# Masks of the closing products from memory and ScalarE instead of ScalarE and GpSimd, in a four-layer graph network

## The chip, the cores and the metric

The kernel runs on one core of one Trainium2 chip. The metric is device time in microseconds. Three runs of the kernel before gave 1397.5, 1397.81 and 1398.58 us; the median is 1397.81.

Each core has a matrix engine (TensorE, PE in the profile, with its weight loads as PEld), VectorE (DVE), ScalarE (ACT), GpSimd (POOL) and SyncE (SP), which here issues the memory transfers. Each engine works through its own queue.

## What is computed

Eight graphs (batches) of 2048 nodes with 64 features pass four layers. They share one adjacency matrix. Layers 0 to 2 are graph attention; each ends in a residual sum and a normalization of every row. Layer 3, the one that the change touches, is attention that works feature by feature:

```python
feat = jax.nn.softplus(x * (INV_SQRT2 * w0[0, 0]) + b0[0])
scores = feat * wa + ba
mask = adj > 0
logits = scores[:, None, :, :] * mask[None, :, :, None].astype(scores.dtype)
logits = jnp.where(mask[None, :, :, None], logits, jnp.float32(-1000000000.0))
attn = jax.nn.softmax(logits, axis=2)
out = jnp.einsum('bijd,bjd->bid', attn, feat)
...
x = _layernorm(x + _L3_gnn_ref(x, L3_gnn_w0, L3_gnn_b0, L3_gnn_wa, L3_gnn_ba, adj), axis=-1)
```

The score of a pair (i, j) depends on j alone, so with d = exp(scores) the output is (mask @ (feat * d)) / (mask @ d): two products of the 0/1 adjacency mask with a narrow matrix.

## The kernel before

**Tiling.** The 2048 nodes are K = 16 blocks of 128. Layers 0 to 2 are worked off as 24 units, one for each layer and batch, in the order of the list `todo`; the last eight are layer 2, and "the last unit" below is layer 2 of batch 7 (named `2_7` in the code). A unit has 16 steps `jb`. In each, VectorE makes a 128 x 2048 tile of weights, ScalarE takes its exponential in layer 2, and TensorE multiplies it.

**Layer 3.** Batches go by pairs (m = 0 to 3). `l3_features(b)` makes the two operands of a batch: softplus on ScalarE (absolute value, exp, log, relu), an addition and the sum `fs` on VectorE, d on GpSimd and ScalarE, then `v`, which holds each operand as a rounded part (copied by ScalarE) and the remainder (subtracted by GpSimd for the first batch of a pair, by VectorE for the second). `l3_products` then works through 64 blocks: block = 16 m + ib is the rows ib of the pair m. A block is 32 matmuls: 16 steps jb times the two parts of `v`, with a 128 x 128 tile of the mask as the stationary operand. ScalarE moves each result from PSUM into `nd`. After every second block `l3_finish` loads the residual (`e`), divides, adds, normalizes and stores to `out`.

**Where the masks come from.** The adjacency lies on chip in eight bits as `edge` (16 x 2048 columns on each partition). The products want it in float32. `mask_out`, from unit 9 on, writes the whole mask in float32 to a buffer in memory, `mask_d`. For blocks 0 to 32, which run beside the units of layer 2, `widen(block)` asks for four quarters, and `fetch()`, called after every fourth step of a block, issues one transfer of 256 KB for a quarter into one of five buffers `mask`. For blocks 33 to 63, behind the last unit (`now[0] == 3`), `widen` casts `edge` on chip into one of two buffers `row`: on ScalarE for even blocks, on GpSimd for odd ones. `widen(block + 1)` is called at the start of `block`, just behind the `nd` of block - 1.

**Order.** PE, VectorE, ScalarE and GpSimd run in the order in which the code issues their instructions (class `InOrder`). The code is a set of generators; `Streams.step` runs each of them to its next `yield`. `l3_products` yields twice in a block, so a block takes two steps, and the steps of the other streams fall between its halves. Behind the last unit these streams are its `finish`, `l3_features` of batches 6 and 7, and `l3_finish` of earlier blocks. SP's transfers are not held to that order: the framework places them in SP's queue.

Of the kernel before, what the change touches and what calls it, by code (L numbers as in the profile page):

```python
# [50 lines left out]
def gnn4_kernel(ctx: ExitStack, tc: tile.TileContext, t, out):  # L51
# [55 lines left out]
    class Banks:  # L107
# [4 lines left out]
        pool = None  # L112
# [28 lines left out]
    pe, dve, act, pool = (InOrder(e) for e in (nc.tensor, nc.vector, nc.scalar, nc.gpsimd))  # L141
# [74 lines left out]
    src = t["L0_gnn_a"]  # L216
# [947 lines left out]
    now = [0, 0, 0]  # L1164
# [82 lines left out]
    def widen(block):  # L1247

        if block >= K * B // 2:
            return  # L1250
        ib = block % K
        src = edge[:, :, ib * P : (ib + 1) * P]
        if now[0] == 3:
            m = work.tile([P, K, P], F32R, tag="row", name=f"mask_{block}")
            if block % 2:
                pool.tensor_copy(m, src)
            else:
                act.copy(m, src)
            wide[block] = [m[:, r * K8 : (r + 1) * K8] for r in range(4)]
            return  # L1260
        wide[block] = [None] * 4
        asked.extend((block, r) for r in range(4))
# [11 lines left out]
    def l3_products():  # L1274

        while len(pairs) == 0 or not hasattr(pairs[0], "v"):
            yield 1
        widen(0)
        for _ in range(4):
            fetch()  # L1280
# [3 lines left out]
        for block in range(K * B // 2):  # L1284
            m, ib = divmod(block, K)
            while len(pairs) <= m or pairs[m].ready < 2:
                yield 1
            q = pairs[m]
            widen(block + 1)
            if ib % K4 == 0:  # L1290
                yield from nd_slots.take()
# [707 lines left out]
```

## Time and profile before

The profiled execution took 1401.63 us, of which the instructions span 1399.8. It is a single execution, 3.8 us above the median of the three timed runs. Times inside the profile count from the start of the span.

| stretch, us | PE busy | DVE busy | ACT busy | POOL busy | granted PE clock | GB/s |
|---|---|---|---|---|---|---|
| 1200 to 1220 | 20.00 | 17.96 | 12.91 | 18.15 | 1.00 | 148 |
| 1220 to 1240 | 15.72 | 10.42 | 16.65 | 11.95 | 0.99 | 88 |
| 1240 to 1260 | 16.54 | 19.36 | 9.43 | 16.02 | 0.84 | 24 |
| 1260 to 1280 | 13.81 | 14.96 | 5.97 | 11.45 | 0.83 | 43 |
| 1280 to 1300 | 12.81 | 16.91 | 12.77 | 14.66 | 0.91 | 21 |
| 1300 to 1320 | 20.00 | 17.37 | 6.98 | 12.14 | 0.91 | 41 |
| 1340 to 1360 | 20.00 | 15.46 | 7.66 | 14.06 | 1.00 | 33 |
| 1380 to 1400 | 5.72 | 11.18 | 1.67 | 7.36 | 0.74 | 34 |

The sums of the last unit end at about 1230.6 us. The table shows four stretches in turn: layer 2 and layer 3 together with PE full; from 1230 to 1300 the last unit's own finish and the features of batches 6 and 7, with PE partly idle; from 1300 to 1386 the products alone with PE full again; and a tail in which the last rows are finished. Over the whole span PE is busy 87%, DVE 86%, ACT 59%, POOL 55%.

All operations of the four compute engines have one line in the profile (L80, the helper that issues them), so instructions are told apart by their tiles. `p_l` is a product of layer 3, `p_o` one of a unit's finish, `p_fm` one with `fs`, `acc` one of an attention unit. `st`, `isw`, `o`, `den`, `nd` and `e` are tiles of finishing; a trailing `_x` marks those of the attention layers.

### The profile page before, as it was taken

The numbers are of one execution on the slowest core, as the hardware profiler recorded it, in microseconds if no ns is written. First come the engines' busy times: TensorE is split into PE (matmuls) and PEld (weight loads), VectorE is DVE, ScalarE is ACT, GpSimd is POOL, SyncE is SP. The second block draws the span as 40 slices with busy tenths as digits, with TensorE's granted clock in tenths as the row PEclk, the third lists the DMA queues.
The fourth block names the chain that finished last, engine by engine and source line by source line (L and its number), as shares of the span: only waits on it lengthen the run. The fifth ranks groups of instructions, "written<-read, shape, count | busy, mean of one in ns | idle before, by whom it ended". The sixth has DMA issues, their size and how long they took to land.

```text
span 1399.8 us, 19531 instructions
## 1 busy us (share of the span) xinstructions
PE 1220.0 (87%) x7169; PEld 624.2 (45%) x7169; DVE 1208.8 (86%) x1108; ACT 821.6 (59%) x1593; POOL 770.2 (55%) x1075
## 2 busy tenths in 40 slices
PE   3699888999898988999997879799989999976995
PEld 3333233333343333333332324256645565666995
DVE  3889889999997999889998888998879798877876
ACT  3444543666646753555547996868666758664432
POOL 1666776546765663645542342443555564776664
PEclk8699999999999999999999988999999899998998
DMA  8640000000000221222101000034543444511111
GB/s 291 228 95 1 1 2 1 1 2 1 3 1 1 91 76 47 78 74 93 32 1 39 1 15 1 22 94 129 146 122 92 127 119 138 160 28 33 35 38 34
DMA packets 112010, 87.24 MB, mean 62 GB/s; under 512 B 57917, under 2 KB 90845, under 8 KB 110882
## 3 DMA queue, kind: packets, MB, share of 16 engines
q1 hardware_dynamic: 111538, 85.79, 20.9%
q8 instruction: 59, 0.97, 0.3%
q14 instruction: 45, 0.37, 0.1%
q10 hardware_dynamic: 368, 0.12, 0.0%
HBM read 60.40 MB, written 25.45 MB: 61 GB/s over the span
## 4 chain that ended last, share of the span: by engine, by line
PE 49%; DVE 24%; ACT 11%; issue 7%; POOL 6%; DMA 2%; SPq 1%; ACTq 0%; DVEq 0%; POOLq 0%
PE acc L80 26%; DVE w L80 16%; PE p_l L80 14%; ACT w L80 2%; PE p_o L80 2%; ACT x L80 2%; DVE o L80 1%; PE r L80 1%; PE p_s L80 1%; POOL sq_x L80 1%; DMA raw<-in_adjT_dram 1%; DVE nd L80 1%; POOL st_x L80 1%; DVE edge L80 1%; ACT y L80 1%
## 5 line engine op out<-in xcount | busy, mean ns | idle before, releaser
L80 DVE SCALAR_TENSOR_TENSOR w<-r,se,edge 128x2048 f32<-128x2048 f32 (+1 forms) x270 | 552.9, 2102 | 30.9 <-PE r L80 22.6
L80 PE MATMUL acc<-w,pv 128*64 128x512 f32 x2048 | 494.1, 615 | 53.0 <-DVE w L80 39.4
L80 DVE SCALAR_TENSOR_TENSOR w<-r,lo_g,edge 128x2048 f32<-128x2048 f32 (+1 forms) x144 | 297.8, 2096 | 26.0 <-PE r L80 12.4
L80 ACT ACTIVATE w<-w,down_g 128x2048 f32<-128x2048 f32 (+1 forms) x144 | 256.8, 1808 | 64.6 <-DVE w L80 57.4
L80 PEld LDWEIGHTS p_l<-v,mask 128*128 128x128 f32 x2048 | 256.3, 196 | 61.8 <-issue 48.5
L80 PE MATMUL p_l<-v,mask 128*128 128x256 f32 x2048 | 271.1, 291 | 10.6 <-POOL mask L80 7.0
L80 PE MATMUL acc<-w,x 128*64 128x512 f32 x1024 | 261.8, 640 | 19.2 <-ACT w L80 16.3
L80 PEld LDWEIGHTS acc<-w,pv 128*64 128x64 f32 x2048 | 132.6, 139 | 307.6 <-issue 182.4
L80 POOL TENSOR_TENSOR sq_x<-sq_x 128x32 f32<-128x32 f32 (+4 forms) x207 | 110.1, 532 | 63.8 <-ACT sq_x L80 49.3
L80 PEld LDWEIGHTS acc<-w,x 128*64 128x64 f32 x1024 | 66.5, 143 | 138.9 <-issue 86.6
L80 ACT ACTIVATE x<-o,st_x 128x64 f32<-128x64 f32 x256 | 91.5, 445 | 13.2 <-POOL st_x L80 13.2
L80 ACT ACTIVATE nd<-p_l,empty 128x256 f32<-128x256 f32 x64 | 30.2, 471 | 109.1 <-PE p_l L80 109.1
L80 ACT ACTIVATE o<-p_o,den 128x64 f32<-128x64 f32 x256 | 55.8, 323 | 47.0 <-DVE den L80 47.0
L80 PE MATMUL p_o<-rh,oT 128*128 128x130 f32 x384 | 61.9, 298 | 24.4 <-DVE o L80 6.7
L80 PEld LDWEIGHTS p_o<-rh,oT 128*128 128x128 f32 x384 | 50.2, 197 | 58.3 <-issue 32.3
L80 ACT COPY oT<-acc 128x512 f32<-128x512 f32 x48 | 25.7, 587 | 80.8 <-PE acc L80 80.8
L80 POOL TENSOR_TENSOR st_x<-isw_x,mhalf 128x16 f32<-128x16 f32 x24 | 70.5, 2938 | 1.9
L80 POOL TENSOR_TENSOR eh<-eh,x 128x1024 f32<-128x1024 f32 (+2 forms) x24 | 36.5, 1532 | 47.0 <-ACT eh L80 47.0
L80 DVE RECIPROCAL nd<-nd 128x256 f32<-128x256 f32 x32 | 55.7, 1742 | 0.0
L80 POOL TENSOR_TENSOR d<-x,wa_bc 128x1024 f32<-128x1024 f32 x8 | 19.0, 2379 | 66.5 <-DVE x L80 66.5
L80 POOL TENSOR_TENSOR sq_x<-o 128x512 f32<-128x512 f32 x23 | 29.3, 1273 | 34.6 <-DVE o L80 34.1
L80 ACT ACTIVATE xs<-x,nodes 128x64 f32<-128x64 f32 x128 | 44.7, 434 | 3.2 <-PE p_xT L80 3.2
(258 smaller groups left out, 1523.5 us busy)
## 6 DMA issues: line engine op xcount, KB each, us to landing
mask<-mask_d SPq DMA_DIRECT2D x132, 256.0 KB
mask_d<-mf SPq DMA_DIRECT2D x32, 512.0 KB
raw<-in_adjT_dram SPq DMA_DIRECT2D x8, 1024.0 KB
raw<-in_adjT_dram SPq DMA_DIRECT2D x16, 512.0 KB
x<-in_x_dram SPq DMA_DIRECT2D x8, 512.0 KB
x_d<-x SPq DMA_DIRECT2D x8, 512.0 KB
e<-x_d SPq DMA_DIRECT2D x64, 64.0 KB
out_dram<-o SPq DMA_DIRECT2D x64, 64.0 KB
```

Of the source, the lines that this page charges most:

```text
L80: ins = f(*args, **kwargs)
```

## The change

Behind the last unit, only odd blocks are cast, and by ScalarE. Even blocks fall through to the four quarters from memory, as blocks 0 to 32 do. So of blocks 33 to 63, the sixteen odd ones move from GpSimd to ScalarE and the fifteen even ones from ScalarE to 60 transfers of 256 KB. `mask_d` holds the whole mask already. The buffers stay as they are: five of `mask`, two of `row`.

```diff
@@ -1250,12 +1250,9 @@
             return
         ib = block % K
         src = edge[:, :, ib * P : (ib + 1) * P]
-        if now[0] == 3:
+        if now[0] == 3 and block % 2:
             m = work.tile([P, K, P], F32R, tag="row", name=f"mask_{block}")
-            if block % 2:
-                pool.tensor_copy(m, src)
-            else:
-                act.copy(m, src)
+            act.copy(m, src)
             wide[block] = [m[:, r * K8 : (r + 1) * K8] for r in range(4)]
             return
         wide[block] = [None] * 4
```

## The prediction

> **What bounds the kernel now.** I read the page, then the chain of waits, then PE's waits and the timelines behind the last unit, where alone the change acts. The chain ends so:
>
> ```profile
> 1297.65 1.80 ACT mask L80
> 1299.49 86.24 PE p_l L80 x704
> ```
>
> From 1299.49 us on TensorE multiplies without a break: 704 matmuls are 22 blocks of 32 (blocks 42 to 63). Then a tail of 14.0 us (1385.8 to 1399.8) finishes the last rows. So PE's work is the bound there, and whatever lets those blocks begin earlier shortens the program. Block 42 was released by a ScalarE cast. Before it, from 1230 to 1300 us, PE waits (columns: total us, times, longest):
>
> ```profile
> PE p_l L80 <- POOL mask L80: 7.0, 2, 6.2
> PE p_o L80 <- DVE st L80: 5.7, 1, 5.7
> PE p_fm L80 <- DVE fs L80: 4.0, 1, 4.0
> PE p_l L80 <- ACT mask L80: 2.3, 1, 2.3
> ```
>
> Casts stand for 9.3 us of the 19 shown, but those 9.3 us are not on offer: PE's queue is in order, and the p_o and p_fm products of the last unit and of batch 6 sit between the blocks. The timeline of PE (start, length, instruction, idle before) shows what lies where:
>
> ```profile
> 1252.24 9.83 PE L80 MATMUL p_l<-v,mask 128*128 128x256 f32 x80
> 1268.26 14.15 PE L80 MATMUL p_l<-v,mask 128*128 128x256 f32 x96 [6.19 <-POOL mask L80]
> 1286.43 0.43 PE L80 MATMUL p_fm<-fs,ones 128*128 128x64 f32 x2 [4.01 <-DVE fs L80]
> 1286.67 5.55 PE L80 MATMUL p_l<-v,mask 128*128 128x256 f32 x32
> 1293.05 4.10 PE L80 MATMUL p_l<-v,mask 128*128 128x256 f32 x32 [0.83 <-POOL mask L80]
> ```
>
> Rows 1 and 2 are blocks 34 (half) to 36 and 37 to 39; p_fm stands before block 40; the last two rows are blocks 40 and 41. Blocks 37 to 39 can come 6 us earlier and PE then only waits longer at p_fm, which needs the sum fs of batch 7's features. So the real chain behind the last unit is not PE but the features of batch 7 on DVE, ACT and POOL.
>
> What the masks cost (min/median/max ns):
>
> ```profile
> L1269 SPq DMA_DIRECT2D mask<-mask_d x132: 319/320/774, 744.5 to 1225.7; - x132
> L80 POOL CAST mask<-edge x16: 1884/1892/2092, 1237.1 to 1378.1; 128x2048 fp32r<-128x2048 fp8e4 x16
> L80 ACT CAST mask<-edge x15: 1882/1889/1896, 1238.6 to 1374.6; 128x2048 fp32r<-128x2048 fp8e4 x15
> ```
>
> ScalarE and GpSimd take the same 1.89 us; it is the place in the queue that differs.
>
> **What the Trainium skill says.** "SBUF — State Buffer", Who interferes with whom: VectorE and GpSimd share a port pair under an exclusive lock, and a VectorE instruction with two SBUF inputs blocks for as long as a GpSimd instruction that reads SBUF runs. The trace agrees: this operation on 16 columns ends with the GpSimd cast of block 37 (1266.33 to 1268.21), while its like in the steady stretch (st, 4 columns) takes 0.15 to 0.25:
>
> ```profile
> 1266.40 1.84 DVE L80 SCALAR_TENSOR_TENSOR st_x<-st_x 128x16 f32<-128x16 f32 x1 [2.37 <-POOL st_x L80]
> 1274.92 2.07 DVE L80 TENSOR_TENSOR o<-o,e 128x256 f32<-128x256 f32 x1
> ```
>
> The second row (0.42 elsewhere) lies under the cast of block 39. "TensorE: Matmul & The Clock Gate", Part 1: after an idle window of some 3.4 us the clock falls to half until PE has been busy as long. The trace has 0.50 granted after the gaps before 1242.7, 1268.3 and 1286.4, and even after the 2.35 us gap before block 42 (1301 to 1304.2): 1.6 us lost each time or more. "DMA: Bandwidth & Descriptors", Anatomy of one DMA: a semaphore wait of a DMA is held on the issuing sequencer, so a fetch queues behind whatever SP waits for; the waits of SP's out_dram issues here are up to 9.1 us.
>
> **The change part by part.** Block 43 is the place to count to, since behind it nothing but PE binds. The order on each engine follows from the streams: one step runs every stream to its next yield, and a block takes two steps.
>
> 1. Fifteen even casts leave ACT (15 x 1.89 = 28 us), sixteen odd ones leave POOL (16 x 1.89 = 30 us) and come onto ACT at their places, just behind the nd of the block two before. Sixty fetches (15 x 4) go onto SP, 0.32 us to issue: 19 us over 150 us of a mostly idle queue. For a landing I have the lone quarter issued at 1225.70: its bytes flow from about 1226.8 to 1228.4, so it lands after 2.7 us, and I take 1.5 us more for each quarter behind it.
>
> 2. Blocks 33 to 36: cast 33 lands behind Relu (ends 1238.2) and is done at 1240.1, before the p_o that holds PE to 1242.67: no cost. Cast 35 runs 1250.5 to 1252.4 and pushes the v copies of batch 6 by 1.89, but POOL was to use them only at 1253.7: nothing. Quarters of 34 at the worst are issued behind the out of 1245.46, at 1246.4, and land from 1249.1 to 1253.6, needed from 1249.95 to 1253.2: 0.4 at most, which point 3 takes up.
>
> 3. Blocks 37 to 39: mask 37 is on ACT behind nd of 35 (1258.3), done 1260.5 instead of 1268.2, so PE runs through and is done with 39 at about 1275. This is given back at p_fm at once. It also pays for any late quarter of 36 or 38 (up to 2 us if SP holds them behind an out): that costs nothing.
>
> 4. The chain to batch 7's features. st_x above loses its blocking: 1.84 to 0.16, gain 1.7. Then o, x_7, the reduction, reciprocal and o follow as before; the add under cast 39 loses 1.6 of its 2.07 and its wait on POOL: done at 1273.85 instead of 1276.99. ScalarE's first softplus, which takes the buffer this add frees, moves from 1277.02 to 1273.9, and fs, hence p_fm, from 1286.43 to 1283.3: 3.1 us. The DVE product under cast 41 (1.85 instead of 0.42) gives 1.4 more: x_7 times d ends at 1290.5 instead of 1295.07, the v copies of batch 7 end at 1292.7 instead of 1297.7.
>
> 5. Block 40 starts at 1283.5, cold after 8 us of idling: 3.84 at full clock plus about 2.2, to 1289.6. Block 41 (its cast is done at 1282.7) to 1293.4. Block 42, from memory, to 1297.3. Its quarters, if behind the e load of 1289.3, land 1292.8 to 1297.3: at most 1.0 late, and hidden by the next wait.
>
> 6. The new wait is block 43. Its cast was on POOL at 1299.05; on ACT it stands behind this one and the nd of block 41:
>
> ```profile
> 1302.65 0.42 ACT L80 ACTIVATE sq<-o 128x256 f32<-128x256 f32 x1 [3.21 <-DVE o L80]
> 1302.97 0.46 ACT L80 ACTIVATE nd<-p_l,empty 128x256 f32<-128x256 f32 x1
> ```
>
> sq waits for DVE's o, which follows four v differences (0.63 to 0.68 each without blocking; the fourth took 2.38 under cast 43). After the copies of 1292.7 and a reciprocal to 1293.3 these end at 1296.0, o at 1296.9, sq 1297.3, nd 1297.75, cast 43 at 1299.65, PE at 1299.8. Block 43 thus starts where 42 started before (1299.49). Before, 42 ended and 43 began at 1305.06. That is 5.3 us gained at full clock. The gap of 2.5 us ahead of 43 equals the one that half-clocked PE before; a second 1.6 us would leave 3.7.
>
> 7. Steady blocks (3.84 us, 7.68 per pair). An odd cast is done 2.3 us after the block two before ends, needed at 3.84: hidden, 1.5 us to spare. Fetches of block 62, say, follow the e load (1369.19, pushed by 1.9 since sq now stands behind a cast; DVE idles 1.78 there and is unblocked by 0.6 per pair): q0 issued 1372, q3 at 1373.3 when its buffer (five deep) is free, landed from 1374.7 to 1379.2, needed from 1378.1 to 1381. Hidden, 1.8 us to spare at the least; without that cover it is up to 2.7 us a pair. The tail keeps its 14 us: the next to last sq waits for nd of block 63 anyway.
>
> Sum: 5.3 less 1.6 with odds of somewhat better than even, plus up to 0.7 from the unblocking of isw under cast 35 earlier in the chain: 4.2 us. The profiled execution is then 1401.63 - 4.2 = 1397.4 (span 1395.6). It stands 3.8 above the median of 1397.81, which I move by the same amount: 1393.6.
>
> **The rivals.**
> - A, more gain: block 43 doesn't wait (sq is ready earlier than I count) and PE goes 40 to 63 without a break; 43 starts at 1297.3, gain 7.8: 1390.0. For it: DVE's rows are full of blocked operations that I shortened only in part. Against it: the v copies and the reciprocal are before sq in any case.
> - B, no effect: PE's lost gap comes back as half clock twice, or the chain is longer by the casts that ACT took over; gain 0 to 2.8, about 1396.5.
> - C, slower: SP holds the fetches. If the queue has each pair's out before the fetches, an out at 1375.28 + 1.9 lets q0 go at 1378.1 and land at 1380.8 against 1378.1, 2.7 us late, on ten even blocks 44 to 62: 27 us less 4.2 is 23 slower, 1420; with 0.8 us each, 1401.5. It decides from 0.42 us a block. For it: SP is in order and its outs wait long. Against it: in the last unit fetches and outs interleave on SP and no wait of PE's for a mask from memory appears; SP's order follows readiness rather than the code (batch 7's store is issued at 1270.66, ahead of the out at 1273.96 that precedes it in the code); in the code's order the fetches are ahead of that out as well.
>
> **How the numbers follow.** The forecast 0.58, A 0.13, B 0.15, C 0.14. About 0.2% (2.8 us) is what a measurement here can tell. The forecast's own range is 1392 to 1395.5. The range asked for reaches over A and B and the near end of C: 1389.0 to 1399.5. Faster by over 0.2%: A and most of the forecast, 0.68. Within: B and the forecast's edge, 0.18. Slower: C, 0.14.
>
> **What would show it.** Right: no wait of PE for POOL; one wait of 4 to 9 us at p_fm, near 1283; a wait of some 2 us for ACT's mask ahead of block 43 near 1300; 21 unbroken blocks behind it; st_x near 0.2 us; the tail at 14 us. Wrong: a wait of PE for a DMA in every second block (C); or p_fm still near 1286, so that the port lock was not what held DVE; or no wait at 43 (A).

## The result, and the profile after

Timed side by side, 22 runs each, the changed kernel has a median of 1395.55 us and the kernel before 1398.03. The ratio of the two sets of runs is 0.9984, 95% interval [0.997, 0.9998], or 2.2 us less (0.3 to 4.2). The forecast was 1393.6 within 1389.0 to 1399.5. A second set of runs, told below, gave 0.9964 [0.9952, 0.9976]. Single runs of either kernel lie anywhere from about 1389 to 1406 us, so the medians need many runs, and the profiles say more than one time does.

The two profiled executions span 1399.8 and 1397.1 us. The code is the same up to the end of the last unit's sums, yet that point lies at 1230.55 us before and at 1231.70 after. From here on I count from it, as +x. Behind it the change took the stretch to the end of the span from 169.25 to 165.4 us: 3.85 less.

The masks (min/median/max ns, first and last start) show that the change is in force: 60 more fetches, none on GpSimd.

```profile
L1266 SPq DMA_DIRECT2D mask<-mask_d x192: 319/320/1020, 744.8 to 1370.9; - x192
L80 ACT CAST mask<-edge x16: 1883/1888/1894, 1239.3 to 1376.1; 128x2048 fp32r<-128x2048 fp8e4 x16
```

PE's waits behind 1230 us (total, times, longest). No wait for GpSimd, none for a mask from memory; one long wait at p_fm, and one for a cast of ScalarE:

```profile
PE p_fm L80 <- DMA e<-x_d: 10.3, 1, 10.3
PE p_o L80 <- DVE st L80: 5.2, 1, 5.2
PE p_l L80 <- ACT mask L80: 2.6, 1, 2.6
...
```

The profile names a load as what p_fm waited for, since that landed last; but p_fm multiplies fs, and the chain below has fs end at 1284.68, just ahead of p_fm at 1284.73. PE's timeline:

```profile
1252.90 21.55 PE L80 MATMUL p_l<-v,mask 128*128 128x256 f32 x176
1284.73 0.69 PE L80 MATMUL p_fm<-fs,ones 128*128 128x64 f32 x2 [10.29 <-DMA e<-x_d]
1285.18 13.21 PE L80 MATMUL p_l<-v,mask 128*128 128x256 f32 x96
1301.01 29.23 PE L80 MATMUL p_l<-v,mask 128*128 128x256 f32 x229 [2.62 <-ACT mask L80]
```

Row 1 is block 34 (half) to 39 without a break; before, 6.2 us were lost in it. They come back in row 2: PE waits 10.3 us at p_fm instead of 4.0. Row 3 is blocks 40 to 42, and block 43 starts in row 4 behind the new wait (the row is cut off where the window shown ends). The chain of waits (start, length, what), which up to the v differences ran through the same places before; there it went on through ScalarE's v copies and `nd` to the cast of block 42:

```profile
1268.02 0.17 DVE st_x L80
...
1281.49 1.23 DVE x L80
1282.74 1.94 DVE fs L80
...
1294.46 2.97 DVE v L80 x4
1297.43 0.35 DVE o L80
1297.87 0.43 DVE o L80
1298.39 0.42 ACT sq L80
1298.81 0.36 ACT nd L80
1299.17 1.79 ACT mask L80
1301.01 82.39 PE p_l L80 x672
```

672 matmuls are blocks 43 to 63: PE is unbroken from one block later than before (there 704, from block 42). Block 43 starts at +69.3, where block 42 started before (+68.9); that is one block of 3.84 us less 0.4. The rest of the 3.85 us lies in the tail behind PE, 13.7 us instead of 14.1. The two VectorE operations that lay under GpSimd's casts are short now (1.84 and 2.07 us before):

```profile
1268.02 0.17 DVE L80 SCALAR_TENSOR_TENSOR st_x<-st_x 128x16 f32<-128x16 f32 x1 [2.37 <-POOL st_x L80]
...
1274.86 0.42 DVE L80 TENSOR_TENSOR o<-o,e 128x256 f32<-128x256 f32 x1
```

These two account for the whole: from the start of st_x to the end of fs the chain took 19.97 us before (1266.40 to 1286.37) and takes 16.66 now (1268.02 to 1284.68), 3.3 us less, and the two operations are shorter by 1.67 and 1.65.

### The profile page after: what moved, and what is told of

Read it like the earlier page. It is cut to its first block, busy times and chain, and to the rows that moved or that the text cites. A ratio compares the mean times of both kernels' runs of the same rounds, so it can differ in the third digit from the quotient of the medians.

```text
span 1397.1 us, 19649 instructions
## 1 busy us (share of the span) xinstructions
PE 1220.7 (87%) x7169; PEld 621.7 (45%) x7169; DVE 1194.6 (86%) x1108; ACT 823.1 (59%) x1594; POOL 735.1 (53%) x1059
## 4 chain that ended last, share of the span: by engine, by line
PE 48%; DVE 24%; ACT 12%; POOL 7%; issue 7%; DMA 2%; SPq 0%; DVEq 0%; POOLq 0%; ACTq 0%
PE acc L80 26%; DVE w L80 16%; PE p_l L80 14%; ACT w L80 3%; PE p_o L80 2%; ACT x L80 2%; DMA raw<-in_adjT_dram 2%; PE r L80 1%; PE p_s L80 1%; DVE o L80 1%; POOL sq_x L80 1%; DVE nd L80 1%; ACT y L80 1%; POOL st_x L80 1%; PE p_h L80 1%
## 5 line engine op out<-in xcount | busy, mean ns | idle before, releaser
L80 PE MATMUL acc<-w,x 128*64 128x512 f32 x1024 | 265.3, 648 | 17.8 <-ACT w L80 15.0
L80 POOL TENSOR_TENSOR st_x<-isw_x,mhalf 128x16 f32<-128x16 f32 x24 | 70.5, 2937 | 1.9
L80 POOL TENSOR_SCALAR isw<-isw 128x4 f32<-128x4 f32 x32 | 8.8, 274 | 105.0 <-DVE isw L80 91.2
L80 DVE RECIPROCAL nd<-nd 128x256 f32<-128x256 f32 x32 | 55.7, 1742 | 0.0
```

What stands on the lines that cost most here:

```text
L80: ins = f(*args, **kwargs)
```

## The experiments

The theory: GpSimd's casts kept VectorE waiting in the chain of batch 7's features, and with that chain shorter the end is set by cast 43 on ScalarE. The rivals: that memory is what pays, by freeing ScalarE; that PE's idle time itself is what costs; that fetches come too late. All kernels below are the changed one with an edit. The stretch is from one profile each, and in the three kernels that were profiled twice it moved by 0.7 to 0.8 us; the ratio, with its interval, is to runs of the kernel before on the same chip.

| kernel | p_fm | stretch, us | ratio to before |
|---|---|---|---|
| before | +55.9 | 169.25 | |
| before, second profile | +55.75 | 168.5 | |
| the change | +53.0 | 165.4 | 0.9984 [0.997, 0.9998] |
| the change, second set | +53.3 | 164.6 | 0.9964 [0.9952, 0.9976] |
| e1: odd on GpSimd | +55.7 | 166.9 | 0.9976 [0.9963, 0.9989] |
| e2: all on ScalarE | +53.2 | 163.3 | 0.9959 [0.9941, 0.9977] |
| e3: 33 to 47 from memory | +53.3 | 175.2 | 1.0032 [1.0019, 1.0045] |
| e4: all from memory | +55.2 | 188.3 | 1.0129 [1.0102, 1.0157] |
| e5: p_fm late | - | 166.2 | 1.0 [0.9989, 1.0011] |
| e7: casts ahead | +52.7 | 161.5 | 0.997 [0.995, 0.9989] |
| e8: p_fm late, 41 and 43 from memory | - | 167.6 | 1.0032 [1.0021, 1.0044] |
| e9: casts ahead, p_fm late | - | 161.5 | 0.9946 [0.992, 0.9973] |
| e9, second set | - | 160.8 | 0.9939 [0.9923, 0.9955] |

The ratios follow the stretches only roughly. e5 and e8 have a shorter stretch than the kernel before, yet e5 is no faster in the timed runs and e8 is slower; the profiled execution of e8 (1393.14 us) is the fastest of its six. What each experiment says of the order of events is read from its profile.

**e1_pool_odd: is it GpSimd's casting or the fetching?**

```diff
-            act.copy(m, src)
+            pool.tensor_copy(m, src)
```

> Even blocks from memory as in the change, odd ones cast by GpSimd as before. Times are counted from the end of the last unit's sums (before: 1230.5 us in the profile, after: 1231.7), where the stretch to the end of the span was 169.3 us before and 165.4 after, and the wait of PE's p_fm ended at +55.9 before and +53.0 after. Theory (the port lock): VectorE is blocked by the casts of blocks 37, 39 and 41 again, st_x takes about 1.8 us, p_fm comes back to about +55.9; block 43 is then released by GpSimd's cast near +70.5 and the stretch is 166 to 168. Rival (the masks from memory alone bring the gain, by taking the cast of block 42 off ScalarE): p_fm stays near +53 and the stretch is 165.4 or less.

Measured: p_fm at +55.7, block 43 at +70.5, stretch 166.9, all three as the theory had it. With GpSimd casting odd blocks, the old length of st_x is back, and PE's waits for GpSimd with it. VectorE's and PE's rows of this kernel:

```profile
1267.71 1.84 DVE L80 SCALAR_TENSOR_TENSOR st_x<-st_x 128x16 f32<-128x16 f32 x1 [2.37 <-POOL st_x L80]
```

```profile
1287.58 0.43 PE L80 MATMUL p_fm<-fs,ones 128*128 128x64 f32 x2 [3.85 <-DVE fs L80]
...
1294.23 7.93 PE L80 MATMUL p_l<-v,mask 128*128 128x256 f32 x64 [0.86 <-POOL mask L80]
1302.39 6.97 PE L80 MATMUL p_l<-v,mask 128*128 128x256 f32 x56 [0.22 <-POOL mask L80]
```

So it is GpSimd's casts that hold p_fm back, with the fetches there or not. Yet this kernel too is faster than before, since block 42 no longer waits for ScalarE and cast 43 stood early enough on GpSimd. The two halves of the change overlap: fetching alone brings 2.3 us of stretch, the whole change 3.85. The difference between e1 and the change is seen in the profiles alone; the timed runs (0.9976 against 0.9984 and 0.9964) do not tell the two apart.

**e2_act_all: is memory needed?**

```diff
-        if now[0] == 3 and block % 2:
+        if now[0] == 3:
```

> No fetch behind the last unit: ScalarE casts odd and even blocks. Theory: the gain of the change is GpSimd casting none; ScalarE has room for both, cast 42 stands behind the copies of batch 7 and ends about 2 us late for PE, but cast 43 is released by the same step of VectorE as in the change, so the stretch from the end of the last unit's sums is 165.4 give or take 0.7, p_fm at about +53. Rival (memory is what pays): PE waits for ScalarE's masks in several blocks and the stretch is 168 or more.

Measured: p_fm at +53.2 as expected, but the stretch is 163.3, 2.1 us better than the theory's number. The rival is out: ScalarE has room for all 31 casts, and taking the casts off GpSimd brings the gain without memory. What the theory's number missed is mostly the clock, some 1.3 of the 2.1 us; block 43 also began 0.6 us earlier, and the tail was 0.3 shorter. PE's last start:

```profile
1291.10 84.97 PE L80 MATMUL p_l<-v,mask 128*128 128x256 f32 x704 [1.37 <-ACT mask L80]
```

22 blocks in 84.97 us are 3.86 each: full clock throughout. Block 42 waited 1.4 us and block 43 not, whereas with the change block 43 waited 2.6 and ran at half clock. The windows of the change (stretch, length, PE busy, granted clock, DMA share, GB/s) show it:

```profile
1301.00:1302.00 1.00, 0.99 (x8) 1.00 0.54 122
1302.00:1303.00 1.00, 1.00 (x7) 0.58 0.53 141
1303.00:1304.00 1.00, 1.00 (x7) 0.50 0.34 83
1304.00:1305.00 1.00, 1.00 (x7) 0.50 0.07 7
1305.00:1306.00 1.00, 1.00 (x8) 0.71 0.44 105
```

**e3_mem_47 and e4_mem_all: how much can be fetched?**

```diff
-        if now[0] == 3 and block % 2:
+        if block >= 48 and block % 2:   # e3
+        if block >= 64:                 # e4
```

> The change, but blocks 33 to 47 all from memory; from 48 on the odd ones are cast by ScalarE. Theory: the wait of 2.6 us for the cast of block 43 and the half clock behind it (about 1.7 us) go, PE runs from p_fm to the last block without a break, the stretch from the end of the last unit's sums is 161 to 162.5. Rival (SP's queue and the fetches limit): 256 KB in each 0.96 us can't be delivered, PE waits for transfers in blocks 40 to 47 and the stretch is 164 to 168.

> No casts at all: all blocks 33 to 63 from memory. The fetches then ask for 1 MB in each 3.84 us, about 273 GB/s, where the layer 2 stretch moved about 160 at a DMA share of 0.55 (an estimate of some 290 GB/s at full share from these two). Theory: fetches are hidden at half that rate but not at this one; PE waits for a transfer in most blocks, 0.3 to 1 us each over 21 blocks, and the stretch is 168 to 185 us. Rival (transfers hide at this rate too): 161 to 163 us.

For e3 my theory was wrong, and the rival's range was too mild: 175.2 us of stretch, PE waiting 15.5 us in eight places for transfers (first row below). e4 has 20 such waits with 24.6 us (second row); its stretch of 188.3 is 3 us over the range that I gave.

```profile
PE p_l L80 <- DMA mask<-mask_d: 15.5, 8, 4.2
```

```profile
PE p_l L80 <- DMA mask<-mask_d: 24.6, 20, 4.4
```

The chain of waits of e3 shows the first of these waits, and that it is the mechanism of my rival C: a store (SP's line 1352) waits on SP for VectorE, the fetch (line 1266) stands behind it, and PE waits for the fetch (DMA):

```profile
1254.42 1.40 DVE o L80
...
1255.84 0.39 SPq L1352
...
1256.27 0.02 SPq L1266
...
1256.32 3.94 DMA mask<-mask_d
...
1260.30 7.60 PE p_l L80 x48
```

Of the later fetches in e3's chain, those issued at 1288.03 and 1322.72 stand behind a load of `e` that waited for VectorE, and the one of 1299.93 follows PE's work, which frees its buffer.

e4 has a second way of losing time: batch 7's features are stored before softplus overwrites them, and among the fetches that store of 512 KB takes 5.77 us, so that ScalarE's x and with it p_fm come 2 us later than with the change:

```profile
1273.22 5.77 DMA x_d<-x
...
1279.02 1.25 ACT x L80
```

In e4's windows (stretch, length, then busy time of PE, PEld, DVE, ACT, POOL, the clock, DMA share, GB/s) the transfer engines are busy 80% of the time:

```profile
1320.00:1340.00 20.00, 16.55 (x132) 15.80 (x131) 9.12 (x21) 2.73 (x6) 5.96 (x10) 1.00 0.80 236
1340.00:1360.00 20.00, 16.67 (x131) 15.82 (x131) 8.98 (x21) 2.73 (x6) 5.97 (x10) 1.00 0.81 245
```

A share of 0.80 at 240 GB/s stands against 0.59 at 168 GB/s in the same stretch of the change, where PE waits for none. SP's own waits in e4 are 60.1 us for a buffer that PE frees (74 times) and 12.1 us for VectorE's o ahead of stores. In the steady part it is the first that counts. The chain there goes from PE, which frees a buffer, over SP's two loads of `e` (line 1331) to a fetch, and back to PE:

```profile
1336.87 3.13 PE p_l L80 x24
...
1340.02 0.32 SPq L1266
...
1340.39 0.42 SPq L1331
...
1341.42 5.57 DMA mask<-mask_d
...
1347.13 5.04 PE p_l L80 x40
```

No store stands in that chain from 1312 to 1357 us, so this is not rival C's mechanism. The five fetches in it took 5.0 to 5.6 us from issue to landing, where the lone one before took 2.7; five buffers of a quarter block each are 4.8 us of PE's work (an estimate, from 3.84 us for a block), so they don't cover such a fetch. Why the fetches take that long, and whether more buffers would help, no run here shows.

**e5_fm_late: does PE's longest wait cost anything?**

```diff
+        if n == "3_7":
+            yield 8
         yield from pm_slots.take()
         p = psum(f"p_fm_{n}")
```

> The change, with the product p_fm of batch 7 issued four blocks later in PE's queue, so that PE's longest wait (10.3 us) is gone. Theory (the end is set by the chain of batch 7's features up to the cast of block 43 on ScalarE): PE does blocks 40 to 42 earlier and then waits for cast 43 as long; block 43 starts at +69 give or take 1 from the end of the last unit's sums, and the stretch from there to the end of the span is 164.5 to 166.5 (165.4 with the change). Rival (PE's idle time at p_fm is what costs): the stretch is 156 to 160.

Measured: stretch 166.2, block 43 at +69.2, as the theory had it. The 10.3 us at p_fm are gone, and the time is spent in other waits, most of it at block 43 (PE's timeline):

```profile
1273.99 4.43 PE L80 MATMUL p_l<-v,mask 128*128 128x256 f32 x24 [3.00 <-DMA mask<-mask_d]
1279.65 6.97 PE L80 MATMUL p_l<-v,mask 128*128 128x256 f32 x56 [1.23 <-ACT mask L80]
1288.54 1.22 PE L80 MATMUL p_l<-v,mask 128*128 128x256 f32 x8 [1.92 <-DMA mask<-mask_d]
1296.52 3.78 PE L80 MATMUL p_l<-v,mask 128*128 128x256 f32 x16 [6.76 <-ACT mask L80]
```

The largest wait of this profile was worth nothing: the cast of block 43 came no earlier for its removal.

**e7_cast_ahead: is cast 43 the wait that decides?**

```diff
-        if block >= K * B // 2:
+        if block >= K * B // 2 or block in wide:
             return
...
             widen(block + 1)
+            if now[0] == 3 and block % 2:
+                widen(block + 2)
```

> The change, with the odd casts issued on ScalarE two blocks ahead instead of one, so that cast 43 stands before the sq that waits for VectorE. Theory (block 43's cast is the wait that took the place of the old ones, 2.6 us, and the half clock behind it costs another 1.7): both go, the stretch from the end of the last unit's sums is 161 give or take 0.7. Rival (another wait, a late transfer for block 42 or 44 or nd, comes in its place): 163.5 or more.

Measured: 161.5, within 0.5 of the theory's number. ScalarE's rows show cast 43 (row 1) ahead of the sq that waits for VectorE (row 2):

```profile
1290.70 1.89 ACT L80 CAST mask<-edge 128x2048 fp32r<-128x2048 fp8e4 x1
1294.64 0.42 ACT L80 ACTIVATE sq<-o 128x256 f32<-128x256 f32 x1 [2.05 <-DVE o L80]
```

PE then has no wait from p_fm to block 63; its last row holds blocks 40 to 63:

```profile
1281.43 94.57 PE L80 MATMUL p_l<-v,mask 128*128 128x256 f32 x768
```

This is the step that shows the new bound: nothing was made cheaper, the odd casts went one block up ScalarE's queue, and that of block 43 with them. The timed runs gained less than the profile promises (0.997; 7.8 us of stretch would be 0.9944), and they do not set e7 apart from the change; why is open.

**e8_fm_late_mem41_43 and e9_cast_ahead_fm_late: can PE's idle time be used?** e8 has e5's edit and `block not in (41, 43)` added to the condition of the cast; e9 has e5's and e7's edits.

> The change, with p_fm four blocks later and blocks 41 and 43 from memory too, so that neither p_fm nor a cast on ScalarE stands between PE and blocks 40 to 44. Theory: if the fetches come in time PE goes on from block 39 with little waiting and the stretch is 150 to 158; from the runs with more blocks from memory, where SP issued fetches behind loads and stores, PE waits for transfers 3 to 8 us in all here, so 155 to 161 is what I take. Rival (fetches of five blocks in a row are as late as in those runs): 163 or more.

> Odd casts two blocks ahead and p_fm four blocks later. Theory: cast 43 still stands behind the copies of batch 7 on ScalarE (about +64.6), so block 43 can start 2 us earlier than with the casts ahead alone, but after a wait of about 5 us and at half clock; stretch 159.5 to 162. Rival (PE's idle time is what costs): 150 to 156.

e8: 167.6, the rival. PE waits 9.9 us in five places for transfers: the fetches of five blocks in a row did not come in time here. The longest of these waits, 2.9 us, has e3's order on SP again: the store of 1281.85 waits for VectorE's o, the fetch behind it takes 4.51 us, and PE goes on at 1287.40. Behind three of the waits, of 2.1 to 2.9 us, PE also ran at half clock. e9: 161.5, as expected, no better than casts ahead alone in the profile. Its waits, though, were not the 5 us for cast 43 that I expected (0.63 there) but two for transfers, 2.85 and 2.94 us.

**before_again, after_again, e9_again: what repeats?**

> The kernel before once more, for a second profile. Theory (what lies ahead of the end of the last unit's sums varies from execution to execution, what lies behind it does not): that point may lie anywhere from 1223 to 1232 us, the stretch behind it is 169.3 give or take 0.6 us, p_fm at +55.9 and block 42 at +68.9. Rival (the stretch itself varies, by where the half clock falls): it differs from 169.3 by more than 1 us.

> The change once more, for a second profile and more timed runs. Theory: stretch 165.4 give or take 0.6 us, p_fm at +53.0, block 43 at +69.3 behind a wait of 2.6 us for ScalarE's cast, the median 1 to 5 us below before. Rival: the stretch is off 165.4 by more than 1 us because the half clock behind block 43's wait isn't there each time (then 163.7).

> Odd casts two blocks ahead and p_fm four blocks later, once more, beside the change. Theory: stretch 161.5 give or take 1, 4 us less than the change, which shows in the median too (ratio to before 0.993 to 0.997). Rival: the waits for transfers that this version shows vary, and the stretch is over 163.

Before: 168.5, p_fm +55.75, block 42 at +68.8, with the sums ending at 1224.7 instead of 1230.55. So 5.8 of the 6.6 us between the two profiles of the kernel before lie ahead of the change, and the stretch itself moved by 0.8, a little more than the 0.6 that the theory allowed. The change: 164.6, which is 0.8 off as well, p_fm +53.3, block 43 at +69.5 behind a wait of 2.1 us. Here the rival has a point: this time PE ran at full clock behind that wait, 21 blocks in 80.89 us, or 3.85 each:

```profile
1295.38 80.89 PE L80 MATMUL p_l<-v,mask 128*128 128x256 f32 x672 [2.14 <-ACT mask L80]
```

against 82.38 us in the first profile. Only about half of these 1.5 us show in the stretch, as block 43 began 0.2 us later and this execution's tail behind PE was longer (14.2 us against 13.7). The version e9, timed twice, has 0.9946 and 0.9939: about 8 us below the kernel before, and below the change.

## Why the prediction was right

The forecast's 4.2 us stand against 3.85 and 3.8 in the two pairs of profiles and against 2.2 and 5.0 (0.0036 of 1397.9) in the two sets of timed runs. The order of events was right; how near the number came is in part luck. The sum as written (5.3, less 1.6 at somewhat better than even odds, plus up to 0.7) gives about 4.4 to 5.1, not 4.2, and its last term came out the other way (point 2). The two pairs of profiles agree better than their parts: PE's last product ended 3.5 us earlier in the first, where the half clock came again, and 4.6 in the second, where it didn't (3.7 and 5.3 by the forecast), while the tail took 0.4 less and 0.8 more. By its own points:

1. *Count to block 43.* Right: behind it PE has no wait in either profile of the change, and block 43 is where the new wait stands. Forecast 1299.8, which is +69.25; measured +69.3 and +69.5.

2. *Blocks 33 to 36 at no cost.* Nearly. Cast 33 ended at +9.5 as worked out. But the v differences that GpSimd took over earlier (it was free of cast 35) now met, by their times, VectorE's o additions, which took 3.38 instead of 2.41 us; st_x began 0.5 us later on this account (+36.3 for +35.85). The 0.7 us that I hoped for from cast 35 went the other way. The isw under that cast did become short, 0.15 instead of 1.26 us, but it was not on the chain: already before, the reciprocal `den` behind it waited 0.23 us for PE's p_o. What moved `den` 0.5 us forward is an earlier p_o, and the o additions then lost 1.0. No run takes this apart.

3. *The gain at 37 to 39 is given back at p_fm.* Right: 6.2 us gone, p_fm's wait grown from 4.0 to 10.3. That is more than the 4 to 9 that I had given as a sign, since block 39 ended at +42.75 and not near +44.45. e5 shows that this idle time costs nothing.

4. *The chain to batch 7's features.* Right in mechanism and nearly in size: p_fm 2.85 us earlier for 3.1 forecast, the v copies done at +62.5 for +62.15. (Before, they ended at 1297.28; my 1297.7 is the end of the `nd` behind them, so 4.6 us were forecast there and 4.2 came.) e1 shows that GpSimd's casts, and not the fetches, hold it; e2 that the same gain comes without memory. What the Trainium skill's "SBUF — State Buffer" (Who interferes with whom) says, that a VectorE operation with two inputs from SBUF waits out a GpSimd one that reads there, is what these rows show: 1.84 us with the cast, in two kernels, and 0.17 without.

5. *Blocks 40 to 42.* Block 42 ended at +66.7; forecast 1297.3, which is +66.75. Here two errors cancel: block 40 began 0.5 us later than reckoned (+53.5), and the cold start cost 1.7 us instead of 2.2.

6. *The new wait at 43.* Right: 2.6 and 2.1 us for 2.5 forecast, and e7 takes it away and gains 3.9 us more of stretch (165.4 to 161.5; 3.1 from the second profile's 164.6). The half clock behind it, which I gave somewhat better than even odds, came in one of the two profiles.

7. *Steady blocks hidden, tail unchanged.* Right: no wait of PE behind block 43, at 168 GB/s; the tail was 13.7 and 14.2 us for 14.0. The last fetch of all, the fourth quarter of block 62, was issued at 1370.9, 4.8 us before that block began, as reckoned (1373.3 and 1378.1). Rival C, slower by late fetches, didn't happen at one block in two. Late fetches are what happens when twice as many are asked for (e4), by 19 us of stretch over the kernel before. The order on SP that I had described for it is seen in the chains of e3 and e8; e4's steady waits come about without it.

The timed runs bear the forecast out less well. The first set is 0.16% down, which is inside the 0.2% to which I gave 0.18, and its median of 1395.55 lies just over the forecast's own range of 1392 to 1395.5; the second is 0.36% down. The part ahead of the change, which differs by 5.8 us between the two profiles of the kernel before, is as large as what was to be measured, and the 1397.81 that I started from is a median of three runs.

## What to carry to other kernels

A long wait on the busiest engine isn't worth its length: ask what stands behind it in the same queue and when that would be ready anyway; here 6 us freed at blocks 37 to 39 and 10 us at p_fm were worth nothing, and casts issued one block earlier in ScalarE's queue were worth 3 to 4 of stretch. When work moves to another engine, look at what it stands behind there, and at whom it kept waiting where it was: casts of the same 1.89 us cost more on GpSimd here, since VectorE waited with them. And moving data through memory for an engine that has room for the work adds a limit: all casts on ScalarE did at least as well as half of them fetched.

## What was not expected of the hardware

The clock behind a short idle gap isn't fixed. The Trainium skill's "TensorE: Matmul & The Clock Gate" (Part 1) gives an idle window of about 3.4 us before the clock falls to half; here shorter gaps brought it down too, and the measurements decide. After gaps of 2.35 us (before, two profiles) and 2.62 (the change) PE fell to half clock for some 3 us; after one of 2.14, in the second profile of the change, and after gaps of 1.35 and 1.37 us in e2, it did not. The length of the gap alone doesn't decide it: in e8 the clock fell after one of 2.12 us. Full and half clock thus differ between executions of one program. Fetches in 256 KB pieces went unnoticed at 168 GB/s and made PE wait at 240 GB/s, with the transfer engines busy 80% of the time and a fetch taking 5.0 to 5.6 us.
